# A list scheduler's cost table replaced, and four gate temporaries handed on in a fixed order

## The chip, the core and the metric

The kernel runs on one core of a Trainium2 chip. Five engines with queues of their own work side by side: PE (matrix products, and beside it PEld, the loading of weights), DVE (VectorE), ACT (ScalarE), POOL (GpSimd) and SP, which here issues the transfers. Each engine takes its instructions in the order in which the program lists them, and an instruction that needs another engine's result waits for a semaphore. The metric is the time of one execution on the device, in microseconds, and lower is better. The profile is of one such execution.

## The reference

Inputs are `x` (128 graphs, 128 nodes, 256 features), `adj` (128 x 128 x 128, 0 or 1) and weights. Two layers, each a normalisation and a residual around a graph network. Cut to what matters:

```python
# layer 0: gated graph network, 3 steps
h = relu(layernorm(x)); A = (adj != 0)
for i in range(3):
    m = h @ weight[i]
    aggr = A^T m                          # per graph
    r, z = sigmoid(aggr @ w_ih.T + h @ w_hh.T + biases)   # parts r and z
    n = tanh(i_n + r * h_n)
    h = (1 - z) * n + z * h
x = x + h
# layer 1: one attention layer
h = relu(layernorm(x)); Wh = h @ W; s = Wh.sum(-1)
e = leaky_relu(s[:, :, None] + s[:, None, :], 0.2), -inf where adj == 0
x = x + softmax(e) @ Wh
```

## The kernel before

**Tiling.** Graphs go in 32 groups of four. A group has three state steps (layers 0, 1 and 2 in the code), and then its attention. The features of a group stand as a tile of 128 partitions x 2 x 512 (`hT`), or by rows of nodes (`rows`).

**One state step.** `edge_sums` adds up the neighbours' states: for each half k of the features a batch of 12 small bf16 matmuls (the states are split into three bf16 parts so that nothing is lost) into a PSUM bank of the tag `misc`, and an ACT copy out of it (L626) into `aT`. `node_sums` forms the sums `hs` and `gs` of blocks (on POOL for the state, on DVE for the edges, L666 to L670) that a multiplication scheme with seven products instead of eight needs. `products` then issues these products on PE (L697; in the third step L711, by rows), into the bank pairs X, Y and Q (`x_rz`, `x_n`, `y_rz`, `y_n`, `q_rz`, `q_n`). Y is emptied three times on the way: `put` (L743, L747, L749, ACT) copies it to the temporaries T2 and T3 in SBUF (tags `t2_rz`, `t2_n`, `t3_rz`, `t3_n`), and `add` (L753, DVE) adds Q to them. The gates (`gru`, L799 to L832, or `gru_rows` in the third step, L849 to L893) read X, Y, T2 and T3. In the third step and from the second group on, states are turned between the two layouts by 16-bit halves: an ACT copy into planes (L559), a DMA transpose on SP's queue (L569), an ACT copy back (L563). `parts_of` and `turned_parts` make the bf16 parts on POOL (L580, L583, L600, L605).

**Attention.** `attention` normalises (L503 to L519), forms the scores on DVE (L1022, L1044 to L1050), takes the exponential on ACT (L1055), turns the matrix by DMA (L1164) and multiplies on PE: `weighted` (L652), then the product with the weights (L1088), two graphs to a `misc` bank, which DVE empties as it updates x (L1097). There are two `misc` banks for everything that isn't a product of the state steps.

**What sets the order.** Nothing runs when it is written. Every operation is handed to `Plan.op` with its engine, a cost in ns, what it reads and writes, and a flag `two` if it uses the ports that DVE and POOL share (all of POOL's have it). `Plan.run` then simulates the engines and gives out one order. At each step it takes, for every engine, those operations that could start first, chooses among them the one with the lowest rank (latest start that still meets all due times behind it), and of the engines the one that starts first. The state products (with `due`) are in `bound`: their order is fixed by their due times, and only other PE work is placed between them. `LAG` is the time between the end of an operation and the start of one on another engine that needs it; for transfers it is the flight. `port` is the time from which the shared ports are free. `MARGIN` (7000) makes work that a product needs urgent 7 us early. Between kinds of buffers there is this difference: a "free" buffer goes to whichever operation comes to it first; a "turn" buffer goes from owner to owner in the order of the steps (`waiting`), and the owner's operations get, by the list `after`, a rank that the next owner's first operation sets. The steps of several groups are interleaved: in the middle of the run a round is layer 0 of group g, layer 1 of g-1 and layer 2 of g-2, with the attention of an earlier group beside them.

Of the kernel before, what the change touches and what calls it, by code (L numbers as in the profile page):

```python
# [13 lines left out]
OP = mybir.AluOpType  # L14
# [3 lines left out]
G = 4  # L18
# [23 lines left out]
class Plan:  # L42
# [7 lines left out]
    LAG = {"PE": 250, "ACT": 300, "DVE": 300, "POOL": 300, "SP": 4000}  # L50
# [20 lines left out]
    def op(self, eng, ns, fn, reads=(), writes=(), room=(), due=None, mark=None,  # L71
           turn=None, two=False, lag=None):
# [24 lines left out]
        for b in free:  # L97
# [3 lines left out]
                           two or eng == "POOL", self.LAG[eng] if lag is None else lag])  # L101
# [4 lines left out]
        if turn is not None:  # L106
            self.turns.append((i, turn))

    def run(self):
# [29 lines left out]
        def rank_all():  # L139
            for i in reversed(topo):  # L140
                eng, ns, due = nodes[i][0], nodes[i][1], nodes[i][5]
                gap = 0 if i in bound else MARGIN
                rank[i] = min([due] + [rank[u] - (0 if nodes[u][0] == eng != "SP" else nodes[i][7])
                                       - (gap if u in bound else 0) for u in after[i]]) - ns
# [15 lines left out]
        clock, port = dict.fromkeys(self.LAG, 0.0), 0.0  # L160
# [3 lines left out]
        while len(order) < len(nodes):  # L164
            best = None
            for e, pool in ready.items():
                if not pool:
                    continue
                starts = []
                for i in pool:  # L170
                    if i in bound and i != chain[-1]:
                        continue
                    t = max(clock[e], at[i], port if nodes[i][6] else 0.0)
                    for b in nodes[i][4]:
                        if b.slot is None:
                            t = max(t, min(slots[b.tag]))
                            if b.tag in waiting and waiting[b.tag][-1] is not b:
                                t = float("inf")
                    starts.append((t, i))
                first = min((t for t, _ in starts), default=float("inf"))  # L180
                if first == float("inf"):
                    continue
                i = min((i for t, i in starts if t <= first), key=lambda i: (rank[i], i))
                if best is None or first < best[0]:
                    best = (first, e, i)
            t, e, i = best
# [4 lines left out]
            clock[e] = t + n[1]  # L191
            if n[6]:
                port = clock[e]
            end = max(end, clock[e])
            for b in n[4]:
# [6 lines left out]
                b.done = max(getattr(b, "done", 0.0), clock[e] + n[7])  # L202
                if not b.left:
                    slots[b.tag][b.slot[1]] = b.done
            for u in users[i]:
                missing[u] -= 1
                at[u] = max(at[u], clock[e] + (0 if nodes[u][0] == e != "SP" else n[7]))
                if not missing[u]:
                    ready[nodes[u][0]].append(u)
# [6 lines left out]
def kernel(  # L216
# [54 lines left out]
        "t2_rz": (1, "free", work, [P, 2, H]), "t2_n": (1, "free", work, [P, 2, H]),  # L271
        "t3_rz": (1, "free", work, [P, 2, H]), "t3_n": (1, "free", work, [P, 2, H]),
# [225 lines left out]
    def normed(src, dst, lo=0, hi=G):  # L498
# [3 lines left out]
        for b in range(lo, hi):  # L502
            op("DVE", 415, lambda b=b: nc.vector.bn_stats(ap(st)[:, b, :], ap(src)[:, b, :]),  # L503
               [(src, b, b + 1)], [(st, b, b + 1)])
# [4 lines left out]
        op("DVE", 160 * (hi - lo), aggr, [st], [mv])  # L509

        def rstd():
# [3 lines left out]
        op("DVE", 170, lambda: nc.vector.scalar_tensor_tensor(  # L515
            ap(nm)[:, part], ap(mv)[:, part, 0], -1.0, ap(rs)[:, part], op0=OP.mult, op1=OP.mult),
           [mv, rs], [nm])
        for b in range(lo, hi):
            op("ACT", 520, lambda b=b: nc.scalar.activation(  # L519
# [31 lines left out]
    def turned_halves(src, rows, dst):  # L551
# [5 lines left out]
        for k in range(KD):  # L557
# [5 lines left out]
            op("ACT", 1340, lambda k=k: nc.scalar.copy(  # L563
# [3 lines left out]
    def transpose(pl, plT, k, n):  # L567

        op("SP", 100, lambda: nc.sync.dma_start_transpose(  # L569
            ap(plT)[:, k, 0:n].rearrange("p c (m q) -> p (c m) q", q=P),  # L570
            ap(pl)[:, k, 0:n].rearrange("p c m -> p (c m)")), [(pl, k, k + 1)], [(plT, k, k + 1)],
           lag=4500)

    def parts_of(rows):
# [3 lines left out]
        for n in range(2):  # L578
            part = slice(2 * n, 2 * n + 2)
            op("POOL", 1106, lambda part=part: nc.gpsimd.tensor_tensor(  # L580
                ap(r1)[:, part], ap(rows)[:, part], top(rows)[:, part], OP.subtract),
               [(rows, 2 * n, 2 * n + 2)], [(r1, n, n + 1)])
            op("POOL", 1050, lambda part=part: nc.gpsimd.tensor_tensor(  # L583
# [5 lines left out]
    def turned_parts(hT):  # L589
# [6 lines left out]
        for k in range(KD):  # L596
# [3 lines left out]
            op("POOL", 1150, lambda k=k, r=r: nc.gpsimd.tensor_tensor(  # L600
# [4 lines left out]
            op("POOL", 1150, lambda k=k, r=r: nc.gpsimd.tensor_tensor(  # L605
# [5 lines left out]
    def edge_sums(parts, a, dst):  # L611
# [5 lines left out]
        for k in range(KD):  # L617
# [7 lines left out]
            op("PE", 700, edges, reads(k) + [a], [ps], [dst])  # L625
# [18 lines left out]
    def weighted(m, a, dst, lo, hi, homes):  # L644

        n, cols = hi - lo, slice(lo * N, hi * N)
        for k in range(KD):
# [7 lines left out]
            op("PE", 225 * n, sums, [(m, lo, hi), (a, lo, hi)], [ps], [dst])  # L655
# [60 lines left out]
    def products(layer, hT, hs, aT, gs, rows=False):  # L716
# [23 lines left out]
        def put(t, y, bias=None, mark=None):  # L740
# [9 lines left out]
            op("ACT", 760, halves, [y, W["bias_n"]], [t], mark=mark)  # L750
# [37 lines left out]
    def gru(layer, hT, hs, aT, gs):  # L788
# [7 lines left out]
        for j, n, src in blocks:  # L796
            cr, cz, cn, i = j, KD + j, 2 * KD + j, 2 * j + n
            s_rz, nn = src["rz"], src["n"]
            op("ACT", 511, lambda j=j, n=n, s_rz=s_rz, c=cr: nc.scalar.activation(  # L799
                view(rz, 0)[:, j, n, :], ap(s_rz)[:, 0, :], AF.Tanh, bias=ap(W["bias_s"])[:, c:c + 1],  # L800
                scale=0.5), [s_rz, W["bias_s"]], [(rz, i, i + 1)])
            if src is X:
                op("DVE", 290, lambda j=j, n=n: nc.vector.tensor_scalar(
                    view(rz, 0)[:, j, n, :], view(rz, 0)[:, j, n, :], 1.0, None, op0=OP.add),
                   [], [(rz, i, i + 1)])
                op("DVE", 480, lambda j=j, n=n, nn=nn: nc.vector.scalar_tensor_tensor(
                    view(u)[:, j, n, :], ap(nn)[:, 0, :], ap(W["bias_n"])[:, 0:1], view(rz, 0)[:, j, n, :],
                    op0=OP.add, op1=OP.mult), [nn, (rz, i, i + 1), W["bias_n"]], [(u, i, i + 1)])
            else:
                op("DVE", 480, lambda j=j, n=n, nn=nn: nc.vector.scalar_tensor_tensor(  # L810
# [6 lines left out]
            op("ACT", 500, lambda j=j, n=n, s_rz=s_rz, c=cz: nc.scalar.activation(  # L817
# [18 lines left out]
    def gru_rows(layer, hT, hs, aT, gs, rows, x1):  # L836
# [6 lines left out]
        for j, n, src in blocks:  # L843
            i = 2 * n + j
            outs = slice(j * P, (j + 1) * P)
            for m, bank in enumerate((src["rz"], src["n"])):
                graph, unit_of = 2 * n + m, 2 * i + m
                sbuf = bank.tag[0] == "t"
                op("ACT", 390, lambda outs=outs, graph=graph, bank=bank: nc.scalar.activation(  # L849
# [3 lines left out]
                op("DVE", 290, lambda outs=outs, graph=graph, bank=bank: nc.vector.scalar_tensor_tensor(  # L853
# [4 lines left out]
                op("DVE", 290, lambda outs=outs, graph=graph, bank=bank: nc.vector.scalar_tensor_tensor(  # L858
                    view(u)[:, graph, outs], view(u)[:, graph, outs], 0.5, flat(bank)[:, 3 * P:4 * P],
                    op0=OP.mult, op1=OP.add), [bank], [(u, unit_of, unit_of + 1)], two=sbuf)  # L860
        for n in (1, 0):
# [5 lines left out]
            tanh = [723, lambda cols=cols: nc.scalar.activation(  # L867
# [19 lines left out]
            op("POOL", 1290, lambda cols=cols, part=part: nc.gpsimd.tensor_tensor(  # L887
# [20 lines left out]
    def group(g):  # L908
# [4 lines left out]
        for t, src, kb in ((rows0, x[graphs].rearrange("b n d -> n b d"), 512),  # L913
                           (at, adj[graphs].rearrange("b n m -> n b m"), 256)):
            if g < TIMED:
                load(t, ap, src, kb, lag=4800 if t is at else 3300)
            else:
                op("SP", 100, lambda t=t, src=src: nc.sync.dma_start(ap(t), src), [], [t])
        op("DVE", 420, lambda: nc.vector.tensor_scalar(ap(a), ap(at), 0.0, None,
                                                       op0=OP.not_equal), [at], [a])  # L920
        plan.due = (phase(g, L - 1) + 2) * SLOT
        normed(rows0, rows0)
        for layer in range(L):
# [9 lines left out]
            else:  # L933
# [3 lines left out]
                op("SP", 100, lambda: nc.sync.dma_start(  # L937
                    ap(x1), x[graphs].rearrange("b n d -> n b d")), [], [x1])
            hs, aT, gs = buf("hs"), buf("aT"), buf("gs")
            node_sums(hT, hs, "POOL", 1390, 940)  # L940
            edge_sums(parts, a, aT)
            node_sums(aT, gs, "DVE", 690, 440)
# [12 lines left out]
    def edges_of(g, a):  # L955

        e = buf("e")
        op("DVE", 415, lambda: nc.vector.tensor_scalar(
            ap(e), ap(a), 0.0, -BIG, op0=OP.is_equal, op1=OP.mult), [a], [e])
        return e, (buf("s_all") if g >= NG - ENDING else e)  # L960

    def attention(g, scores, x1, h1, lo, hi):
# [8 lines left out]
        for b in range(lo, hi):  # L971
            hw = buf("hw")
            op("DVE", 520, lambda b=b, hw=hw: nc.vector.scalar_tensor_tensor(
# [65 lines left out]
        if ending:  # L1039
            op("DVE", cost, lambda: nc.vector.tensor_reduce(small(top), sums(), AX.X, OP.max), units, [top])  # L1040
            op("DVE", 260, bound, [s], [top, low])
            op("ACT", 320 * n, leaky, [s] + units, [(e, lo, hi)])
# [17 lines left out]
        op("ACT", (400 if ending else 320) * n, exps, [low],  # L1060
# [39 lines left out]
        op("SP", 100, lambda: nc.sync.dma_start(  # L1100
# [35 lines left out]
    def by_graph(g, lo, hi, exps, e, low, den, rden, rows_w, x1):  # L1136
# [3 lines left out]
        for b in range(lo, hi):  # L1140
            i = b - lo
            op("ACT", 400, lambda b=b: exps(b, b + 1), [low], [(e, b, b + 1), (den, b, b + 1)])
# [12 lines left out]
            op("SP", 100, lambda b=b: nc.sync.dma_start(out[g * G + b], ap(x1)[:, b]), [(x1, b, b + 1)], [])  # L1155
# [4 lines left out]
    def turned_halves_of(halves, src, dst):  # L1160
# [3 lines left out]
        op("SP", 100, lambda: nc.sync.dma_start_transpose(  # L1164
            ap(peT).rearrange("p two g q -> p (two g) q"),
            ap(pe).rearrange("p two g m -> p (two g m)")), [pe], [peT])
        op("ACT", 1340, lambda: nc.scalar.copy(halves_of_blocks(dst), ap(peT)), [peT], [dst])
# [36 lines left out]
```

## Time and profile before

| | us |
|---|---|
| three runs | 2105.02, 2105.40, 2105.88 |
| their median | 2105.40 |
| span of the profiled execution | 2103.8 |
| PE, time in which some matmul is under way | 2084.5 |
| PE, first matmul starts | 1.25 |

The profiled span runs from the first to the last instruction of the program, and what lies around it is part of the time of a run, so the two differ by 1.6 us. A matmul instruction of 128 x 256 in f32 shows a duration of 0.38 us, but one starts every 0.216 us, since they overlap; one of 128 x 384 starts every 0.323 us, a bf16 one of 128 x 128 every 0.056. So a PE that is busy all the time may still not be full, and the starts are what counts. Every f32 product appears as two instructions.

In the middle of the run the pattern repeats with each round of three state steps. The page's busy shares of an engine are over the whole span; for a question about one place, the stretch tables (busy us of each engine between two times) and the chain of waits are of more use. "Waits" give the engine and line that waited, the one waited for, the sum in us, how often, and the longest.

### The profile page before, as it was taken

To read this page: it belongs to the slowest core of one execution; us is meant where nothing else is said; L and a number is where in the kernel's file an instruction comes from. 1 tells how busy PE (TensorE), PEld (TensorE's weight loads), DVE (VectorE), ACT (ScalarE), POOL (GpSimd) and SP (SyncE) were. 2 spreads that over 40 slices of the span, in tenths; PEclk is the share of its full clock that TensorE was granted. 3 is DMA by queue.
4 is the path that set the end of the run, shared out by engine and by line. 5 is a ranking of instruction groups with operands and counts; after the bars stand their busy time and mean duration, and the time that the engine had idled before them with its cause. 6 is when DMAs were issued, how large, how long until landed. Compare 5 with 4: busy or idle time off the path is not lost.

```text
span 2103.8 us, 30718 instructions
## 1 busy us (share of the span) xinstructions
PE 2084.5 (99%) x10624; PEld 1661.6 (79%) x10624; DVE 1714.1 (81%) x3626; ACT 1612.9 (77%) x2977; POOL 923.7 (44%) x881
## 2 busy tenths in 40 slices
PE   8999999999999999999999999999999999999998
PEld 6886887777887778887778877778877788688765
DVE  6767888788888888888888887888878978778788
ACT  5577887877878787877778777778787777677676
POOL 4544554344443435543444543444444454335330
PEclk9999999999999999999999999999999999999999
DMA  4322323322233222323223233222323222312231
GB/s 131 61 51 48 56 54 81 67 54 61 68 73 81 60 58 65 72 70 76 61 56 70 68 73 68 54 61 68 74 61 85 45 62 71 76 41 61 56 71 41
DMA packets 365148, 137.02 MB, mean 65 GB/s; under 512 B 296384, under 2 KB 364736, under 8 KB 364992
## 3 DMA queue, kind: packets, MB, share of 16 engines
q1 hardware_dynamic: 364992, 135.05, 28.8%
q8 instruction: 84, 1.38, 0.3%
q14 instruction: 72, 0.59, 0.1%
HBM read 45.36 MB, written 16.78 MB: 30 GB/s over the span
## 4 chain that ended last, share of the span: by engine, by line
PE 94%; DVE 3%; ACT 1%; DMA 1%; issue 0%; SPq 0%; DVEq 0%; ACTq 0%
PE y_rz L697 15%; PE q_rz L697 10%; PE x_rz L697 10%; PE y_n L697 8%; PE misc L623 6%; PE y_n L711 5%; PE y_rz L711 5%; PE x_n L697 5%; PE q_n L697 5%; PE misc L1088 5%; PE q_rz L711 4%; PE x_n L711 4%; PE x_rz L711 4%; PE q_n L711 4%; PE misc L652 3%; PE misc L452 0%
## 5 line engine op out<-in xcount | busy, mean ns | idle before, releaser
L580 POOL TENSOR_TENSOR r<-rows 128x512 f32<-128x512 f32 x126 | 139.7, 1129 | 295.9 <-ACT rows L563 201.7
L743 ACT COPY t_rz<-y_rz 128x512 f32<-128x512 f32 x192 | 112.5, 586 | 130.4 <-PE y_rz L697 91.8
L666 POOL TENSOR_TENSOR hs<-hT 128x512 f32<-128x512 f32 x96 | 126.6, 1319 | 190.7 <-PE y_n L711 110.9
L753 DVE TENSOR_TENSOR t_rz<-t_rz,q_rz 128x512 f32<-128x512 f32 x192 | 131.5, 685 | 86.5 <-ACT t_rz L743 43.5
L697 PE MATMUL y_rz<-hs,s_hh 128*128 128x256 f32 x768 | 197.4, 379 | 0.6 <-ACT t_rz L743 0.5
L697 PE MATMUL y_rz<-gs,s_x 128*128 128x256 f32 x768 | 197.1, 379 | 0.0
L670 POOL TENSOR_TENSOR hs<-hT,hs 128x256 f32<-128x256 f32 x96 | 77.5, 807 | 209.6 <-PE q_n L711 169.2
L697 PEld LDWEIGHTS y_rz<-gs,s_x 128*128 128x128 f32 x768 | 145.9, 190 | 19.8
L605 POOL TENSOR_TENSOR pl<-d,pl 128x512 bf16<-128x512 f32 x64 | 76.1, 1193 | 191.9 <-ACT pl L603 191.7
L697 PEld LDWEIGHTS y_rz<-hs,s_hh 128*128 128x128 f32 x768 | 143.5, 190 | 20.0 <-ACT t_rz L743 1.4
L583 POOL TENSOR_TENSOR p<-r 128x512 bf16<-128x512 f32 x126 | 156.7, 1262 | 0.0
L753 DVE TENSOR_TENSOR t_n<-t_n,q_n 128x512 f32<-128x512 f32 x192 | 131.2, 683 | 30.4 <-PE q_n L711 13.0
L666 DVE TENSOR_TENSOR gs<-aT 128x512 f32<-128x512 f32 x96 | 87.8, 914 | 54.3 <-ACT aT L626 53.7
L697 PE MATMUL x_rz<-aT,s_x 128*128 128x256 f32 x512 | 131.4, 379 | 0.0
L697 PE MATMUL x_rz<-hT,s_hh 128*128 128x256 f32 x512 | 131.4, 379 | 0.0
L600 POOL TENSOR_TENSOR d<-hT,pl 128x512 f32<-128x512 f32 x64 | 82.6, 1293 | 97.2 <-ACT pl L598 91.5
L626 ACT COPY aT<-misc 128x512 f32<-128x512 f32 x190 | 110.4, 586 | 17.7 <-PE misc L623 13.0
L1088 PE MATMUL misc<-w,uT 128*128 128x256 f32 x480 | 115.1, 383 | 3.1 <-DVE x L1097 2.3
L697 PE MATMUL y_n<-hs,s_hh 128*128 128x256 f32 x384 | 114.3, 379 | 0.0
L697 PE MATMUL y_n<-gs,s_x 128*128 128x256 f32 x384 | 114.2, 379 | 0.0
L697 PEld LDWEIGHTS x_rz<-hT,s_hh 128*128 128x128 f32 x512 | 97.2, 190 | 19.3
L887 POOL TENSOR_TENSOR x<-x,u 128x512 f32<-128x512 f32 x60 | 79.4, 1342 | 69.8 <-DMA x<-in_x_dram 42.1
(286 smaller groups left out, 6324.4 us busy)
## 6 DMA issues: line engine op xcount, KB each, us to landing
rows<-in_x_dram SPq DMA_DIRECT2D x32, 512.0 KB, 4.2
x<-in_x_dram SPq DMA_DIRECT2D x32, 512.0 KB, 3.9
out_dram<-x SPq DMA_DIRECT2D x31, 512.0 KB, 2.9
at<-in_adj_dram SPq DMA_DIRECT2D x32, 256.0 KB, 2.8
plT<-pl SPq DMA_TRANSPOSE x186, 3.3
peT<-pe SPq DMA_TRANSPOSE x60, 3.1
e<-in_L_gnn_weight_dram SPq DMA_DIRECT2D x3, 256.0 KB, 3.1
rz<-in_L_gnn_w_ih_dram SPq DMA_DIRECT2D x2, 384.0 KB, 4.3
```

The lines of the kernel that those rows point to most:

```text
L580: op("POOL", 1106, lambda part=part: nc.gpsimd.tensor_tensor(ap(r1)[:, part], ap(rows)[:, part], top(rows)[:, part], OP.subtract), [(rows, ...
L583: op("POOL", 1050, lambda part=part: nc.gpsimd.tensor_tensor(ap(p3)[:, part], ap(r1)[:, part], top(r1)[:, part], OP.subtract), [(r1, n, n ...
L600: op("POOL", 1150, lambda k=k, r=r: nc.gpsimd.tensor_tensor(ap(r), ap(hT)[:, k], part(pl, k, 0), OP.subtract), [(hT, 2 * k, 2 * k + 2), (p ...
L623: nc.tensor.matmul(flat(ps)[:, b * N:(b + 1) * N], part(i, b, k), ap(a)[:, b, :], start=(i == 0), stop=(i == 2))
L626: op("ACT", 590, lambda k=k, ps=ps: nc.scalar.copy(ap(dst)[:, k, :], flat(ps)), [ps], [(dst, 2 * k, 2 * k + 2)])
L666: op(eng, cost, lambda: sub(ap(w)[:, 0:2, :], blocks()[:, 1::2, :], blocks()[:, 0:2, :], OP.subtract), [t], [(w, 0, 2)], two=True)
L697: nc.tensor.matmul(ap(bank)[:, half, :], ap(w)[:, i - 1, gate, :], source(i, t, sums), start=(first and c == 0 and m == 0), stop=False, sk ...
L711: op("PE", 645, lambda c=c, w=w, t=t, sums=sums: nc.tensor.matmul(flat(bank)[:, c * P:(c + 3) * P], source(i, t, sums)[:, m * N:(m + 1) * ...
L743: op("ACT", 590, lambda: nc.scalar.copy(ap(t), ap(y)), [y], [t], mark=mark)
L753: op("DVE", 690, lambda: nc.vector.tensor_tensor(ap(t), ap(t), ap(q), OP.add), [q], [t])
L887: op("POOL", 1290, lambda cols=cols, part=part: nc.gpsimd.tensor_tensor(part(x1), part(x1), ap(u)[:, cols], OP.add), [(u, 2 * lo, 2 * hi)] ...
L1088: nc.tensor.matmul(ap(ps)[:, b, :], ap(uT)[:, k, (m + b) * N:(m + b + 1) * N], ap(w1)[:, k, :], start=(k == 0), stop=(k == KD - 1))
```

## The change

The edit replaces the numbers with which the planner thinks, changes its rules in four places, and turns the four temporaries from "free" to "turn". The arithmetic and the set of instructions stay; what can differ is their order and in which of two equal buffers something stands.

1. Lags: `LAG` of an operation becomes what passes before its result is there (PE 163, SP 3600, 0 for the others), and `SIGNAL` adds the time that the waiting engine takes to see it. New `Plan.wait(i, u)` joins them; only between two PE operations is it zero, so operations of one engine that depend on each other have a gap too.
2. `OVER`: an engine is free for its next operation before the one under way is done (ACT 103 ns, DVE 84, POOL 42).
3. `thin` and `FLIP`: a PE operation that isn't thin starts 56 ns later behind one that is. The bf16 batches of `edge_sums` are thin.
4. `HANDOFF`: the shared ports are free 120 ns before an operation on them is done; and among engines that could start at the same time, the one whose operation asked first gets the turn.
5. Costs of single operations, and more DVE operations marked as users of the ports (`two`): L515, L803, L919 and L958.
6. Transfers: a transpose costs SP 1283 with a flight of 2200 (before 100 and 4500), other transfers 480 (before 100); the few timed loads at the start keep theirs.

```diff
-    LAG = {"PE": 250, "ACT": 300, "DVE": 300, "POOL": 300, "SP": 4000}
+    LAG = {"PE": 163, "ACT": 0, "DVE": 0, "POOL": 0, "SP": 3600}
+    OVER = {"PE": 0, "ACT": 103, "DVE": 84, "POOL": 42, "SP": 0}
+    FLIP, HANDOFF = 56, 120
+    SIGNAL = {"PE": 53, "ACT": 36, "DVE": 36, "POOL": 78, "SP": 28}
...
+    def wait(self, i, u):
+
+        a, b = self.nodes[i], self.nodes[u][0]
+        return 0 if a[0] == b == "PE" else a[7] + self.SIGNAL[b]
...
-                rank[i] = min([due] + [rank[u] - (0 if nodes[u][0] == eng != "SP" else nodes[i][7])
+                rank[i] = min([due] + [rank[u] - self.wait(i, u)
                                        - (gap if u in bound else 0) for u in after[i]]) - ns
...
-                    t = max(clock[e], at[i], port if nodes[i][6] else 0.0)
+                    t = max(clock[e] + (self.FLIP if thin and e == "PE" and not nodes[i][8] else 0), at[i])
...
-                    starts.append((t, i))
-                first = min((t for t, _ in starts), default=float("inf"))
+                    starts.append((max(t, port) if nodes[i][6] else t, t, i))
+                first = min((t for t, _, _ in starts), default=float("inf"))
...
-                i = min((i for t, i in starts if t <= first), key=lambda i: (rank[i], i))
-                if best is None or first < best[0]:
-                    best = (first, e, i)
-            t, e, i = best
+                asked, i = min(((r, i) for t, r, i in starts if t <= first), key=lambda x: (rank[x[1]], x[1]))
+                if best is None or (first, asked) < best[:2]:
+                    best = (first, asked, e, i)
+            t, _, e, i = best
...
-            clock[e] = t + n[1]
+            done = t + n[1]
+            clock[e] = done - self.OVER[e]
             if n[6]:
-                port = clock[e]
-            end = max(end, clock[e])
+                port = done - self.HANDOFF
+            if e == "PE":
+                thin = n[8]
+            end = max(end, done)
...
-                b.done = max(getattr(b, "done", 0.0), clock[e] + n[7])
+                b.done = max(getattr(b, "done", 0.0), done + n[7] + 36)
...
-                at[u] = max(at[u], clock[e] + (0 if nodes[u][0] == e != "SP" else n[7]))
+                at[u] = max(at[u], done + self.wait(i, u))
...
-        "t2_rz": (1, "free", work, [P, 2, H]), "t2_n": (1, "free", work, [P, 2, H]),
-        "t3_rz": (1, "free", work, [P, 2, H]), "t3_n": (1, "free", work, [P, 2, H]),
+        "t2_rz": (1, "turn", work, [P, 2, H]), "t2_n": (1, "turn", work, [P, 2, H]),
+        "t3_rz": (1, "turn", work, [P, 2, H]), "t3_n": (1, "turn", work, [P, 2, H]),
...
-        op("SP", 100, lambda: nc.sync.dma_start_transpose(
+        op("SP", 1283, lambda: nc.sync.dma_start_transpose(
...
-           lag=4500)
+           lag=2200)
...
-            op("PE", 700, edges, reads(k) + [a], [ps], [dst])
+            op("PE", 671, edges, reads(k) + [a], [ps], [dst], thin=True)
...
-                op("DVE", 480, lambda j=j, n=n, nn=nn: nc.vector.scalar_tensor_tensor(
+                op("DVE", 422, lambda j=j, n=n, nn=nn: nc.vector.scalar_tensor_tensor(
```

The other costs, line by line (before, after; `n` is the number of graphs): L503 415, 412; L508 160n, 85+65n; L515 170, 155; L519 520, 592; L563 and L1167 1340, 1347; L580 1106, 1042; L583 1050, 1042; L600 and L605 1150, 1158; L652 225n, 223n; L747 with L749 760, 728; L799 511, 496; L803 290, 278; L806 480, 485; L817 500, 495; L849 390, 403; L853 and L858 290, 286; tanh in `gru_rows` (L867) 723, 630; L887 1290, 1273; `node_sums` on POOL 1390 and 940, then 1272 and 730, its halves on DVE 440, 426; L958 415, 420; L973 520, 432; L1031 320n, 100+285n; L1055 320n (400n in the last two groups), 100+290n (100+390n); the exponential of the last group, by graph, 400, 480; L918, L937, L1100 and L1155 100, 480.

## The prediction

> **What bounds the kernel now.** I read the page first (busy shares, then the slices), then stretches of 64 us, then the waits of PE, and last the chain of waits in the one stretch that stood out.
>
> The busy shares of the page:
>
> ```profile
> PE 2084.5 (99%) x10624; PEld 1661.6 (79%) x10624; DVE 1714.1 (81%) x3626; ACT 1612.9 (77%) x2977; POOL 923.7 (44%) x881
> ```
>
> The stretches (length, then busy time of PE, PEld, DVE, ACT, POOL, clock, DMA share, GB/s):
>
> ```profile
> 0.00:64.00 64.00, 58.38 (x303) 46.51 (x304) 45.09 (x98) 38.84 (x80) 36.38 (x42) 1.00 0.40 113
> ...
> 615.72:679.58 63.86, 63.86 (x330) 51.23 (x329) 51.18 (x116) 51.05 (x95) 26.46 (x27) 1.00 0.33 71
> 679.58:743.44 63.86, 63.86 (x330) 51.23 (x329) 54.38 (x112) 49.65 (x91) 30.31 (x29) 1.00 0.29 66
> ...
> 1796.00:1815.00 19.00, 14.63 (x41) 8.91 (x40) 15.79 (x31) 9.39 (x19) 5.54 (x4) 0.82 0.33 97
> ...
> 2048.00:2104.00 56.00, 48.27 (x218) 32.63 (x216) 45.78 (x140) 35.08 (x86) 6.48 (x8) 0.98 0.17 48
> ```
>
> The reader is to see two things. A round of three state steps takes 63.86 us, and PE is busy in all of them: in the middle of the run there is no hole to close, and the change takes no matmul away. And holes are in few places: 5.6 us in the first 64, 7.7 in the last 56, 4.4 in the 19 us from 1796, where the clock is also below full. The longest waits of PE say the same:
>
> ```profile
> PE misc L1088 <- DVE x L1097: 2.3, 1, 2.3
> PE y_n L711 <- ACT t_n L743: 2.0, 1, 2.0
> PE misc L533 <- DVE h L360: 1.3, 1, 1.3
> PE misc L441 <- DMA e<-in_L_gnn_weight_dram: 1.3, 1, 1.3
> ```
>
> The first two belong to the stretch at 1796; its chain of waits (start us, us, what) shows why:
>
> ```profile
> 1793.78 1.15 DVE gs L670
> 1794.92 1.18 DVE u L810
> 1796.10 0.61 DVE e L1022
> 1796.71 0.02 issue
> 1796.74 1.54 DVE e L1044
> ...
> 1798.30 1.54 DVE e L1046
> ...
> 1801.59 3.66 PE misc L1088 x8
> ```
>
> VectorE works through the attention scores in order, and the update of x (L1097) that frees the misc bank for PE stands behind them. L810 takes 0.42 us elsewhere in this stretch and L1044 0.76 on the mean of 30; here they take twice that or more, beside GpSimd's L580, L583 and L600.
>
> **What the Trainium skill says.** "SBUF — State Buffer", section "Who interferes with whom": a VectorE instruction with two SBUF inputs and a GpSimd instruction that reads SBUF share ports, and the later one blocks wholly. The 1.54 us above agrees, and so does L1048, a reduction with one input, at 0.69 us beside them. "TensorE: Matmul & The Clock Gate", section "What's actually happening": the clock falls to half after an idle window of about 3.4 us and comes back after a busy one. Here two stretches of 3.3 us (from 1801.8 and 1808.7) show 0.50, after waits of only 2.35 and 2.03 us, so a shorter wait is enough. No page bears on an f32 matmul behind a bf16 one; the trace gives that below.
>
> **The change part by part.**
>
> *Matmul flips (thin, FLIP).* In the PE timeline the first f32 matmul behind a bf16 batch is 53 to 56 ns longer (median 55); there are 148 such places, 8.2 us in all. An edge sum is two batches of 12, k=0 and k=1, and often a product stands between them. The planner now charges 56 ns to whatever follows a thin batch unless it is thin too, so a ready thin batch goes first whatever its rank. Following the planner's dependencies through the trace, at 50 of the 148 places the next thin batch already had its inputs and its bank. 50 x 56 ns = 2.8 us less, on PE itself, so nothing hides it. Bounds: 0, if banks are held longer in the new order, and 148 x 56 = 8.3. I take 2.8. The product that steps back does so by 0.67 us (12 x 56 ns), beside full work on PE.
>
> *The jam at 1796.* It costs 2.35 + 2.03 us of waiting; the eight L1088 take 3.65 us and not 1.89 (1.76 more), the x and n products after it 1.48, 1.48 and 1.17 and not 0.81 each (1.70 more). Sum 7.8 us. The new planner knows VectorE's and GpSimd's durations better (L810 from 480 to 422, L1044 as before, L580 from 1106 to 1042), gives the port up 120 ns before an operation ends, gives it to the one that asked first, and marks L515, L803, L919 and L958 as users of it. It also lets a VectorE instruction start 84 ns before the one ahead is done and an ACT one 103, so that side work is planned earlier (in the VectorE timeline L810 does start at 1789.68, 80 ns before L832, begun at 1789.07 and 0.69 long, ends). A jam that needs four port collisions in a row is an accident of one order; in a re-made order I expect it gone more often than not. Bounds: 7.8 gained, or none; I take 7.8. If it goes, what is late next is the q_rz product at 2033 (0.7 us), which I leave.
>
> *Lags.* ACT and DVE results were planned 300 ns late, now 36 or, to PE, 53. The trace supports this: where PE waited, it started 52 to 55 ns after the releaser ended. No instruction is added, and a cover of 0.25 us that the order had for free goes. In the round from 615.72, the closest release is that of y_rz at 642.13: its bank was emptied by an ACT copy that ended at 641.69, so 0.44 us early; the next ones are 0.9 and 1.1. I cost this at nothing, covered by those margins; without them, see the slower rival.
>
> *DMA.* A transpose was planned as 100 + 4500 ns, now 1283 + 2200 and 36 for the signal, 3.52 us. The trace has 3.0, 3.3 and 5.1 us (least, median, most) for the 186 of plT. All are on SP's queue, which also carries the rows, adjacency and output transfers; each SP step now holds its queue 480 or 1283 ns in the plan, as it does on the chip (a transpose's issue takes 1.27). The reading copies (L563, L1167) stand in ACT's queue; one that is early blocks the bank-emptying copies behind it, by up to 5.1 - 3.5 = 1.6 us. Nothing for the median, and for the slow tenth (over 4.0 us) 0.5 us, about the smallest margin. I take 0, with 0 to 10 us (0.45 in each of 23 rounds) as bounds.
>
> *Set order for t2/t3.* Each of the four is one buffer and in use by one step at a time; steps are already made in the order of their phases, so the hand-over sequence is the same. New is that VectorE's and ACT's work that frees a buffer takes its urgency from the next step that writes it. No instruction, no wait on PE that is not there now: 0, with 1 us either way as bounds, about one more or one fewer of the waits of 0.7 to 1.3 us that PE has now.
>
> *The two ends.* The first 64 us wait for weights and first rows, the last 56 for the last group's softmax. Both are chains of data; I take 0, with 2 us either way for each.
>
> Sum: 2103.8 - 2.8 - 7.8 = 2093.2 us span. The three runs of before have a median of 2105.4, 1.6 above the profiled span, so **2094.8**.
>
> **Rivals.**
>
> A, the forecast (0.52): flips and jam go. 2089 to 2099, from the ends' 2 us each and two new waits of about 2.
>
> B, the jam stays or another of its size takes its place (0.22): 2105.4 - 2.8 = 2102.6. For it: DVE has 81% and the last groups run in another order of phases, where ports collide most; nothing in the change moves the attention chain off VectorE. Against it: one case in the trace.
>
> C, slower (0.20): the evictions become late in every round. Place: ACT's copies of the y banks (L743) behind a transpose copy that waits, and PE's y products behind them. The smallest margin is 0.44 us; a copy later by 1.4 leaves PE waiting 0.95 in each of the 23 like rounds between 300 and 1760 us: 21.9 us. With A's 10.6 gained: 2105.4 + 11.3 = 2116.7. It cancels the gain from 0.46 us a round (10.6 / 23), and is slower by more than can be mistaken from 0.64. For it: landings up to 5.1 us and the planned 300 ns gone. Against: ACT is busy 51 of 63.86 us, and 90% of the landings come within 4.0.
>
> D, it does not do what it says (0.06): the fixed order of products carries the rest, the batches stay apart, the jam stays: 2105.4.
>
> **How the numbers follow.** The smallest difference that a measurement of this kernel can tell from none is 0.2%, 4.2 us: faster is below 2101.2, slower above 2109.6. Faster: 0.50 of A and 0.07 of B (another small stall gone beside the flips), 0.57. Same: 0.02 of A, 0.13 of B, D, and 0.01 of C, 0.22. Slower: 0.02 of B and 0.19 of C, 0.21. The range is 2088 to 2110: it takes in A, B and D with their unknown costs, and leaves out most of C (0.17) and 0.03 below. Likeliest alone: 2089 to 2099.
>
> **What would show it.** Flips: 95 to 100 places where f32 follows bf16, with the k=0 and k=1 batches as one group of 24 in the timeline, and rounds of about 63.75 us. Jam: PE busy throughout 1780 to 1830, clock 1.00. C: PE's waits show L743 ahead of y products 20 times or more, and PE in a middle round below 63.8 busy us. I am wrong if PE's holes move to the middle of the run, or if a wait of over 2 us and a half clock stand anywhere between 64 and 2040.

## The result and the profile after

The changed kernel takes 2112.7 us (median of five runs, 2111.3 to 2113.3), the kernel before 2105.0 beside it: a ratio of 1.0038, interval 1.0026 to 1.0050. It is slower, where 2094.8 was forecast. Its profiled span is 2110.9 us, 7.0 longer than before.

The busy shares of its page, then the stretch tables (from and to, length, busy time of PE, PEld, DVE, ACT, POOL, clock, DMA share, GB/s):

```profile
PE 2084.3 (99%) x10624; PEld 1658.4 (79%) x10624; DVE 1680.2 (80%) x3626; ACT 1594.6 (76%) x2977; POOL 921.5 (44%) x881
```

```profile
0.00:64.00 64.00, 59.02 (x304) 47.34 (x305) 44.43 (x97) 37.86 (x80) 38.82 (x45) 1.00 0.38 108
647.06:711.83 64.77, 64.09 (x329) 51.14 (x328) 53.01 (x112) 49.86 (x93) 28.36 (x27) 1.00 0.28 65
711.83:776.61 64.78, 64.07 (x329) 51.13 (x328) 53.03 (x112) 49.85 (x93) 28.37 (x27) 1.00 0.29 66
1780.00:1830.00 50.00, 50.00 (x266) 39.21 (x265) 39.56 (x82) 43.47 (x80) 27.77 (x25) 1.00 0.23 45
2048.00:2110.00 62.00, 56.42 (x250) 38.51 (x248) 48.26 (x157) 38.17 (x93) 4.66 (x8) 1.00 0.18 53
```

The page's shares look like those of before, and would hide the change. The stretches don't: the jam near 1800 us is gone, with PE busy throughout and the clock at 1.00, but a round in the middle takes 64.78 us instead of 63.86, with a hole of 0.7. The waits of PE name it:

```profile
PE y_rz L722 <- ACT t_rz L754: 14.1, 19, 1.3
PE q_n L1160 <- DVE eT L1158: 1.4, 1, 1.4
```

(Lines have moved by 7 to 11: L722 is L711 of before, the product of the third step by rows; L754 is L743, the copy that empties a Y bank.) It comes in 19 of the 20 rounds between 300 and 1600 us.

A full account comes from the starts of PE's matmuls: the distance from each start to the next, less that of an unhindered one of its shape (0.216 us for 128 x 256, 0.323 for 128 x 384, 0.056 for bf16, 0.112 and 0.429 for the f32 ones of 128 and 512 columns). What is left over, in us, with the flips apart:

| | before | after | e1_swap | e5_split | e10_split553 |
|---|---|---|---|---|---|
| flips (f32 behind bf16) | 8.1 | 5.5 | 5.5 | 5.5 | 5.4 |
| 0 to 64 us | 8.6 | 9.3 | 10.4 | 10.6 | 8.2 |
| 64 to 300 | 1.1 | 1.2 | 2.0 | 0.9 | 0.3 |
| 300 to 1600 | -1.5 | 20.2 | 1.9 | 0.9 | -1.5 |
| 1600 to 2000 | 9.3 | 0.3 | 0.5 | 0.3 | -0.4 |
| 2000 to the last matmul | 8.2 | 4.6 | 4.5 | 5.1 | 3.8 |
| ahead of the first and behind the last | 5.6 | 5.3 | 5.3 | 6.1 | 5.3 |
| span | 2103.8 | 2110.9 | 2094.5 | 2093.8 | 2085.6 |

(A little below zero is in the shapes' medians. The three columns on the right are experiments.) So the change gained 2.6 us of flips, 9.0 between 1600 and 2000, and 3.9 at the end, and lost 21.7 in the rounds and 0.8 before them: 7.0 in sum.

Why the copy is late is read from one round. ACT's timeline before the wait at 648.22 us (start, length, instruction; the bracket is idle time of the engine and who ended it):

```profile
643.51 0.72 ACT L834 ACTIVATE u<-u,bias_i 128x512 f32<-128x512 f32 x1 [1.40 <-DVE u L825]
644.14 0.57 ACT L668 COPY uT<-misc 128x512 f32<-128x512 f32 x1
644.61 2.08 ACT L530 ACTIVATE h<-x,nm,rs 128x256 f32<-128x256 f32 x4
646.64 1.04 ACT L570 COPY pl<-hT 128x1024 uint16<-128x1024 uint16 x1
647.59 0.58 ACT L754 COPY t_rz<-y_rz 128x512 f32<-128x512 f32 x1
```

VectorE's and then GpSimd's timeline in the same round, and PE's:

```profile
641.87 1.28 DVE L679 TENSOR_TENSOR gs<-gs,aT 128x256 f32<-128x256 f32 x1
643.07 0.41 DVE L825 SCALAR_TENSOR_TENSOR u<-u,t_n 128x256 f32<-128x256 f32 x1
643.40 0.41 DVE L681 TENSOR_TENSOR gs<-aT,gs 128x256 f32<-128x256 f32 x1
```

```profile
641.71 1.16 POOL L616 TENSOR_TENSOR pl<-d,pl 128x512 bf16<-128x512 f32 x1 [2.40 <-ACT pl L614]
```

```profile
648.22 0.91 PE L722 MATMUL y_rz<-s_hh,hs 128*128 128x384 f32 x2 [0.68 <-ACT t_rz L754]
```

GpSimd's L616 began 0.16 us ahead of VectorE's L679, which takes 1.28 us here, while L681, of the same shape, takes 0.41 shortly after. Behind it comes L825, ACT's tanh (L834) waits for that, and behind the tanh stand 3.7 us of work (L668, four L530, L570) that PE's next product doesn't need; only then comes the copy that it waits for. Every link of this is an engine's own order.

But this meeting was in the plan. `Plan.run` gives each operation a start (`t` in its code), and these starts can be set beside the trace, operation by operation. Just ahead of the wait PE runs 11.04 us behind its planned times; "on PE's count" below is a planned time plus that. The plan has L679 wait behind L616 and end at 642.26 on PE's count. It ended at 643.15, so VectorE was 0.9 us late, but it had been so before: the tanh of 635.97 is 0.92 late. What the plan did not have lies ahead of that tanh, on GpSimd and VectorE:

```profile
633.15 1.45 POOL L677 TENSOR_TENSOR hs<-hT 128x512 f32<-128x512 f32 x1
634.68 1.06 POOL L679 TENSOR_TENSOR hs<-hs,hT 128x256 f32<-128x256 f32 x1
```

```profile
633.40 1.75 DVE L840 SCALAR_TENSOR_TENSOR d<-rz,d 128x512 f32<-128x512 f32 x1
635.52 0.42 DVE L825 SCALAR_TENSOR_TENSOR u<-u,y_n 128x256 f32<-128x256 f32 x1
635.86 1.23 DVE L843 SCALAR_TENSOR_TENSOR hT<-d,u 128x512 f32<-128x512 f32 x1
```

```profile
635.97 0.72 ACT L834 ACTIVATE u<-u,bias_i 128x512 f32<-128x512 f32 x1 [1.60 <-DVE u L825]
```

GpSimd's first node sum of the state (L677) was planned behind VectorE's L840, at 634.10 on PE's count; it began 0.95 us sooner, ahead of L840. L840 and L843, planned at 0.69 us each, took 1.75 and 1.23 beside the sums. From there on VectorE and ACT stay about 0.9 us late. And the plan has only 0.15 us between the end of the copy (L754) and the start of the product (L722), 0.05 of it for the signal.

### The profile page after: what moved, and what is told of

Its sections match the earlier page's. It is cut to its first block, busy times and chain, and to the rows that moved or that the text cites. A ratio compares the mean times of both kernels' runs of the same rounds, so it can differ in the third digit from the quotient of the medians.

```text
span 2110.9 us, 30632 instructions
## 1 busy us (share of the span) xinstructions
PE 2084.3 (99%) x10624; PEld 1658.4 (79%) x10624; DVE 1680.2 (80%) x3626; ACT 1594.6 (76%) x2977; POOL 921.5 (44%) x881
## 4 chain that ended last, share of the span: by engine, by line
PE 79%; ACT 10%; DVE 7%; issue 2%; DMA 0%; POOL 0%; SPq 0%; DVEq 0%; ACTq 0%; POOLq 0%
PE y_rz L708 14%; PE x_rz L708 10%; PE q_rz L708 8%; PE y_n L708 7%; PE y_rz L722 5%; PE misc L1099 5%; PE y_n L722 5%; PE misc L634 5%; PE x_n L708 4%; PE q_n L708 4%; PE q_rz L722 3%; PE x_n L722 3%; PE x_rz L722 3%; PE q_n L722 3%; ACT h L530 2%
## 5 line engine op out<-in xcount | busy, mean ns | idle before, releaser
L677 POOL TENSOR_TENSOR hs<-hT 128x512 f32<-128x512 f32 x96 | 129.5, 1350 | 304.5 <-PE y_n L722 238.9
L754 ACT COPY t_rz<-y_rz 128x512 f32<-128x512 f32 x192 | 112.2, 584 | 146.4 <-PE y_rz L708 136.1
L708 PE MATMUL y_rz<-hs,s_hh 128*128 128x256 f32 x768 | 200.0, 383 | 1.0 <-ACT t_rz L754 0.9
L708 PE MATMUL y_rz<-gs,s_x 128*128 128x256 f32 x768 | 197.1, 379 | 0.0
L708 PEld LDWEIGHTS y_rz<-hs,s_hh 128*128 128x128 f32 x768 | 142.8, 190 | 27.1 <-ACT t_rz L754 9.2
L708 PEld LDWEIGHTS y_rz<-gs,s_x 128*128 128x128 f32 x768 | 145.9, 190 | 19.8
L681 POOL TENSOR_TENSOR hs<-hT,hs 128x256 f32<-128x256 f32 x96 | 75.3, 785 | 177.1 <-PE q_n L722 160.7
L834 ACT ACTIVATE u<-u,bias_i 128x512 f32<-128x512 f32 x128 | 92.8, 725 | 74.0 <-DVE u L825 73.8
L708 PE MATMUL x_rz<-hT,s_hh 128*128 128x256 f32 x512 | 131.4, 379 | 0.0
L708 PE MATMUL x_rz<-aT,s_x 128*128 128x256 f32 x512 | 131.4, 379 | 0.0
L840 DVE SCALAR_TENSOR_TENSOR d<-rz,d 128x512 f32<-128x512 f32 x128 | 117.6, 920 | 0.9
L637 ACT COPY aT<-misc 128x512 f32<-128x512 f32 x190 | 102.8, 581 | 18.1 <-PE misc L634 17.9
L616 POOL TENSOR_TENSOR pl<-d,pl 128x512 bf16<-128x512 f32 x64 | 75.7, 1183 | 89.9 <-ACT pl L614 89.8
L708 PE MATMUL y_n<-gs,s_x 128*128 128x256 f32 x384 | 114.3, 379 | 0.0
L708 PE MATMUL y_n<-hs,s_hh 128*128 128x256 f32 x384 | 114.3, 379 | 0.0
L837 DVE TENSOR_TENSOR d<-hT,u 128x512 f32<-128x512 f32 x128 | 107.3, 839 | 8.5 <-ACT u L834 6.3
```

Source lines behind the costliest of these rows:

```text
L637: op("ACT", 590, lambda k=k, ps=ps: nc.scalar.copy(ap(dst)[:, k, :], flat(ps)), [ps], [(dst, 2 * k, 2 * k + 2)])
L677: op(eng, cost, lambda: sub(ap(w)[:, 0:2, :], blocks()[:, 1::2, :], blocks()[:, 0:2, :], OP.subtract), [t], [(w, 0, 2)], two=True)
L708: nc.tensor.matmul(ap(bank)[:, half, :], ap(w)[:, i - 1, gate, :], source(i, t, sums), start=(first and c == 0 and m == 0), stop=False, sk ...
L754: op("ACT", 590, lambda: nc.scalar.copy(ap(t), ap(y)), [y], [t], mark=mark)
L837: op("DVE", 690, lambda j=j, d=d, cols=cols: nc.vector.tensor_tensor(ap(d), ap(hT)[:, j, :], ap(u)[:, cols], OP.subtract), [(hT, lo, hi), ...
L840: op("DVE", 690, lambda d=d, cols=cols: nc.vector.scalar_tensor_tensor(ap(d), ap(rz)[:, 1, cols], 1.0, ap(d), op0=OP.add, op1=OP.mult), [( ...
```

## The experiments

All ran beside the kernel before, whose median in the three sets was 2102.7, 2104.5 and 2103.0 us. Edits are to the changed kernel unless said otherwise. Theory S: the copies are planned without room, so any lateness of VectorE reaches PE. Its rivals: D, transposes that land late (rival C of the prediction); T, the set order of the temporaries; and P, which says where VectorE's lateness is from.

**The suspected order alone (e1_swap).** At the end of `run`:

```diff
+        for q, p in zip(acts, acts[1:]):
+            if nodes[q][1] == 1045 and nodes[p][1] == 590 and any(b.tag == "t2_rz" for b in nodes[p][4]) \
+                    and all(order_at[u] > order_at[p] for u in users[q]):
+                order.remove(q)
+                order.insert(order.index(p) + 1, q)
```

> The changed kernel with one edit of its order: where ACT's copy into the planes (1045 ns, of the turned halves) stands just ahead of the copy that empties y_rz into t2_rz, it goes behind it. Theory S (the T2 copy is planned just in time behind other ACT work, and VectorE's lateness passes through it to PE): the waits of PE's y_rz product on that copy (0.7 us and a slow restart, 18 times) go, rounds fall from 64.8 to 63.7-63.9 us, the time to about 2095 (2093 to 2099). If the copy is late for its own input (PE's earlier y product, or a DMA ahead of it), the swap changes nothing: 2112.

Measured: 2095.5 us, ratio 0.9963 (0.9948 to 0.9978). A round, and ACT's timeline at the place:

```profile
644.70:708.50 63.80, 63.80 (x329) 51.17 (x329) 51.95 (x113) 49.69 (x93) 28.56 (x27) 1.00 0.30 66
```

```profile
641.96 0.72 ACT L841 ACTIVATE u<-u,bias_i 128x512 f32<-128x512 f32 x1 [1.40 <-DVE u L832]
...
645.03 0.57 ACT L761 COPY t_rz<-y_rz 128x512 f32<-128x512 f32 x1
645.50 1.05 ACT L577 COPY pl<-hT 128x1024 uint16<-128x1024 uint16 x1
```

The tanh still waits 1.40 us for VectorE; only the copy stands one place earlier, and the waits are gone. The edit makes this exchange 24 times, about once in a round. One instruction of ACT, 1.05 us long and ahead of the copy, cost 16.4 us of the span over the run (2110.9 to 2094.5). That the copy stood behind it without room is the shown cause of the loss; why VectorE was late is the next question.

**The set order undone (e2_free).** The four tags "free" again.

> The changed kernel with the four temporaries as before (free instead of in turn), the new numbers kept. Theory T (the set order gives VectorE's and ACT's work a new urgency, and that put other work ahead of the copy): the wait at the y_rz product goes, about 2095. Theory S: the numbers cause it, and just-in-time copies appear with either kind of buffer, at the same place or another: 2105 to 2120, with waits of 0.3 to 1.5 us in each round.

Measured: 2124.3 us, ratio 1.0102 (1.0087 to 1.0117). The waits move to the Y products of the first two steps (L708):

```profile
PE y_rz L708 <- ACT t_rz L754: 17.8, 22, 3.4
```

Theory T falls: without the set order it is the same kind of wait at another place, and the time is longer, by 11.6 us between the medians (which are of different sets) and by 14.4 between the profiled spans.

**More room for PE (e3_signal1053).** `SIGNAL = {"PE": 1053, ...}`.

> The changed kernel with SIGNAL to PE 1053 instead of 53: everything PE needs is planned to be there 1 us earlier. Theory S: VectorE runs 0.9 to 1.2 us later than planned, so 1 us of planned slack takes up nearly all of it: PE's waits in the rounds shrink to under 0.2 us, time 2094 to 2099. Theory D (late transposes): landings up to 1.6 us over plan; waits shrink but some of 0.5 us stay, 2098 to 2105. Theory T: no change, 2110 to 2114.

Measured: 2099.6 us, ratio 0.9984 (0.9977 to 0.9992), just outside S's 2094 to 2099. In the rounds no wait is left (the account has -1.3 us from 300 to 1600). Theory S holds there; the total is dulled by a wait of 5.0 us for VectorE's gs sums near 2030 us, with a stretch at half clock behind it (the pair after the wait takes 1.65 us instead of 0.81), which the new order brought.

**Transposes as before (e4_transposes).** 100 with a flight of 4500 instead of 1283 and 2200.

> The changed kernel with the transposes' cost and flight as before (100 + 4500 ns instead of 1283 + 2200). Theory D (rival C as the prediction put it: ACT's reading copies wait for transposes that land later than planned): the wait at the y_rz product goes, 2094 to 2099. Theory S: ACT doesn't wait for transposes there; the order is another one, but PE's waits in the rounds stay of the same kind, 2105 to 2120.

Measured: 2118.6 us, ratio 1.0070 (1.0053 to 1.0089). PE's waits:

```profile
PE y_rz L722 <- ACT t_rz L754: 10.7, 22, 0.8
PE y_rz L708 <- ACT t_rz L754: 3.8, 10, 0.5
```

The wait stays at the same product. D's expectation fails: transposes planned as late as before don't take the wait away.

**GpSimd's starts known to the planner (e5_split).** In this kernel `hs` is one tile of four blocks. The planner holds a buffer until its last reader is done, and the last reader is the last product of a step; but the first node sum writes two blocks alone, whose readers are done several products earlier, and on the chip it starts then. (In the changed kernel the sum of 608.94 us began 0.12 us after the last reader of its two blocks had ended, and 5.1 us ahead of the end of the tile's last reader.) With three tiles of the same bytes the planner sees what the chip does:

```diff
-        "hs": (2, "turn", work, [P, 4, H]), ...
-        "gs": (2, "turn", work, [P, 4, H]),
+        "hs": (2, "turn", work, [P, 2, H]), "hs2": (2, "turn", work, [P, 1, H]),
+        "hs3": (2, "turn", work, [P, 1, H]), ...        # and gs, gs2, gs3 alike
-        op(eng, cost, lambda: sub(ap(w)[:, 0:2, :], ... [t], [(w, 0, 2)], two=True)
+        op(eng, cost, lambda: sub(ap(w[0])[:, 0:2, :], ... [t], [w[0]], two=True)
```

> The changed kernel with each of hs and gs in three tiles (two, one and one of its four blocks) instead of one, the same bytes and the same operations. The planner keeps a buffer taken until its last reader is done, while on the chip GpSimd may write the first two blocks as soon as their own readers are; with three tiles it plans with that. Theory P (GpSimd starts its sums earlier than planned, meets VectorE at the shared ports at times nobody planned, and that makes VectorE late): VectorE's late steps in the round get fewer, and the wait at the y products falls from 0.87 us with its restart to under 0.3, time 2094 to 2101. If the lateness has another source, waits of 0.5 to 1.3 us a round stay somewhere: 2105 to 2120.

Measured: 2094.6 us, ratio 0.9949 (0.9932 to 0.9965). The page, and ACT at the same place of the round:

```profile
PE 2078.7 (99%) x10624; PEld 1663.6 (79%) x10624; DVE 1615.4 (77%) x3626; ACT 1594.7 (76%) x2977; POOL 916.8 (44%) x881
```

```profile
639.26 0.58 ACT L670 COPY uT<-misc 128x512 f32<-128x512 f32 x1 [1.28 <-PE misc L665]
639.75 2.08 ACT L532 ACTIVATE h<-x,nm,rs 128x256 f32<-128x256 f32 x4
641.73 1.04 ACT L572 COPY pl<-hT 128x1024 uint16<-128x1024 uint16 x1
642.80 0.58 ACT L756 COPY t_rz<-y_rz 128x512 f32<-128x512 f32 x1
```

The four instructions stand in the same order as in the changed kernel, and yet PE doesn't wait. It is another order all the same: the tanh (L836, at 636.76) now stands well ahead of them, and nothing near them waits for VectorE. Meetings at the ports are not gone either: VectorE's first gs sum of this round (636.91) takes 1.27 us, but the plan has it wait there. The same 3626 VectorE instructions are busy 64.8 us less (1680.2 to 1615.4). Reductions with one input keep their length (L1074 of the changed kernel 684 ns, L1076 here 685), while one with two inputs from SBUF falls from 920 ns (L840) to 719 (L842), so this is less time spent waiting at the ports.

Plan and trace side by side, from 300 to 1600 us and for operations of a single instruction, show what the split did (times in us, on PE's count; "tight" are the copies of Y to T2 that the plan lets end less than 0.2 ahead of a y_rz product of the third step):

| | changed kernel | e1_swap | e5_split |
|---|---|---|---|
| tight copies in the plan, and the median distance to the product | 20, 0.15 | 20, 0.15 | 19, 0.18 |
| their end against the plan, median | 0.96 late | 0.07 early | 0.27 early |
| GpSimd's first sum of the state ahead of its plan, median | 5.1 | 4.9 | 0.0 |
| VectorE operations ended over 0.5 late | 797 of 2002 | 1050 of 2027 | 84 of 2028 |

(The plan of e1_swap is the one ahead of its exchange.) The plan is as tight in all three. In e1_swap VectorE is as late as ever, and the copy in time because it was moved; in e5_split GpSimd starts as planned, and VectorE and the copy are in time. So theory P holds for the changed kernel: node sums that GpSimd began ahead of the plan made VectorE late. Two things had to come together, a plan without room and a start that the plan had wrong.

**Room for ACT's results alone (e6_act1000).** `wait` gets 1000 ns more from ACT to PE.

> The changed kernel with 1000 ns more between ACT's results and PE alone (53 stays from VectorE and GpSimd). Theory S: the y copies are what is planned too tightly, so the rounds are free of waits as with 1053 for all, and the 5 us wait for VectorE's gs sums near the end of that run needn't be there: 2091 to 2097. If VectorE's results are too tight for PE as well, waits for DVE show up in the rounds: 2098 to 2110.

Measured: 2102.5 us, ratio 0.9991 (0.9985 to 0.9998). The rounds are as free of waits as in e3 (-1.3 us from 300 to 1600), but 7.3 us are lost from 64 to 300 and 11.2 at the end. The part on the rounds holds, the time (2091 to 2097) doesn't.

**The flips alone (e7_thin_only).** The kernel before with `thin` and `FLIP`.

> The kernel before with thin and FLIP alone. Flips fall from 148 to about 100, 2.7 us less on PE. Theory S: with the old lags of 250 to 300 ns the rounds have no wait, 63.7 us each; the jam near 1800 us may stay or go: 2102 with it, 2094 without. If pairing the edge batches itself makes the y copies late, rounds are 64 us or more: over 2107.

Measured: 2100.7 us, ratio 0.9983 (0.9975 to 0.9990). Flips cost 6.3 us instead of 8.1, less of a gain than in the full change; the rounds are clean (-1.2), and the jam is gone (1.7 from 1600 to 2000). In its place a product waits 2.5 us for ACT near 2053. The time is still not the 2094 expected without the jam: 4.0 us are lost from 64 to 300 us (1.1 before) and 9.4 at the end (8.2 before). So pairing the batches did no harm in the rounds, and a small edit to the planner was enough for an order without the jam.

**The old lags (e8_lag_old).** `LAG` of before, `OVER`, `HANDOFF` and `SIGNAL` zero, the rest of the change kept.

> The changed kernel with LAG as before (250, 300, 4000), OVER, HANDOFF and SIGNAL at zero, the new costs, thin, the marks of port users and the set order kept. Theory S: 300 ns of planned lag on ACT's and VectorE's results, and the operations planned without overlap, leave room again; waits in the rounds under 0.3 us, 2094 to 2103. If the new costs or marks made the order tight, waits at the y products stay: 2106 to 2120.

Measured: 2121.0 us, ratio 1.0077 (1.0062 to 1.0092). This was a miss. The Y copies no longer stand first, but 18.9 us are lost from 300 to 1600 at the misc banks, to ACT's copies (L637) and VectorE's updates (L1108). The old lags with the new costs and marks make another order, worse in another way; which of them does it isn't shown. S's expectation failed here, and since the waits are mostly at other places, the run tells little on the copies.

**The split without the change (e9_before_split).** The kernel before, with the tiles of e5.

> The kernel before with hs and gs in three tiles each, as in the run e5_split, and nothing else. If the jam near 1800 us came from GpSimd's unplanned starts, it goes: 2096 to 2098 (7.8 less, flips stay at 148). If it is an accident of the order whatever the planner knows of GpSimd, the order changes and the time lies anywhere from 2096 to 2110. VectorE's busy time against before: theory P expects it lower (under 1690 us).

Measured: 2107.8 us, ratio 1.0026 (1.0016 to 1.0036). VectorE is busy 1716.4 us, not less than before (1714.1), and the stretch from 1600 to 2000 loses 9.1 us as it did, in another wait: 5.9 us of a y_rz product for its copy, at 1777. P's expectation for VectorE missed here. With the old numbers the split doesn't make the plan right: GpSimd's first sum of the state still begins over 0.5 us ahead of it in 44 of 61 cases between 300 and 1600 us. And something else than the jam's wait can cost the same at that place.

**Both remedies (e10_split553).** e5 with `SIGNAL` to PE 553.

> e5_split with SIGNAL to PE 553 instead of 53. Theory S and P together: with GpSimd planned well, VectorE is at most 0.1 us later than planned at the y copies, so half a microsecond of room is enough and takes away the one wait of 0.7 left at 325 us: 2092 to 2095. If the room costs more at the end of the run than it saves in the rounds (as the 5 us wait with 1053 did): 2095 to 2100.

Measured: 2087.0 us, ratio 0.9923 (0.9907 to 0.9940), faster than expected and the fastest of all. Page and one round:

```profile
PE 2074.6 (99%) x10624; PEld 1662.1 (80%) x10624; DVE 1592.3 (76%) x3626; ACT 1594.7 (76%) x2977; POOL 924.1 (44%) x881
```

```profile
640.00:703.70 63.70, 63.70 (x330) 51.25 (x329) 48.29 (x112) 49.91 (x93) 28.98 (x27) 1.00 0.29 67
```

How much room the copies have is seen from the other side, ACT's waits for the third step's Y product (sum, times): where ACT waits for PE, the copy is in time. Before, after, and in this run:

```profile
ACT t_rz L743 <- PE y_rz L711: 37.8, 42, 4.5
```

```profile
ACT t_rz L754 <- PE y_rz L722: 9.9, 12, 2.1
```

```profile
ACT t_rz L756 <- PE y_rz L724: 52.9, 44, 3.4
```

The change took this from 42 times to 12, half a microsecond of planned room with the split gave 44. In this plan no copy of Y to T2 or T3 is tight in the third step any more: the least distance there is 1.77 us between 300 and 1600.

**The split without the set order (e11_split_free).**

> e5_split with the four temporaries free as before. If the set order is worth nothing of its own once GpSimd is planned well: 2093 to 2097. If it is what keeps the y copies in time (with one tile hs it was 2124 without it): waits at y_rz in the rounds, 2105 to 2125.

Measured: 2100.6 us, ratio 0.9987 (0.9980 to 0.9994), between the two expectations: 6.0 us over e5 between the medians of two sets, 4.4 between the profiled spans, 8 if each is set against the kernel before that ran beside it. With the split, too, the kernel with the set order is the faster one, by less than without it (11.6 and 14.4, e2 against the changed kernel). How much of this is the set order and how much the accident of a new order isn't shown.

## Why the prediction was wrong

*Flips: right.* 2.8 us forecast, 2.6 measured, at 100 places left of 149.

*The jam: right in size, thin in reason.* 7.8 us forecast, 9.0 gained from 1600 to 2000. That it is an accident of one order is borne out: of the twelve orders run (e1_swap left out), four others (e2, e4, e8, e9) lose 4 to 12 us in the same stretch, and seven lose 3 or less. That it went is thus partly luck. One reading of the lines was wrong: L1048 was named as a one-input reduction that keeps its 0.69 us beside GpSimd's work, but it began at 1799.86, when GpSimd's L600 had ended (1796.01 and 3.27 us) and L605 not yet begun (1804.04), so it shows nothing on the ports.

*Lags: the step that failed.* "I cost this at nothing, covered by those margins". The margins of 0.44, 0.9 and 1.1 us were read off the order of before and treated as if they stayed while the lags shrank. They don't belong to the kernel but to the order. The smallest was for the most part the lag itself: the plan of before has 0.38 us between that copy and its product, of which 0.30 is the old `LAG` of ACT. Without that lag nothing keeps 0.30 us free, and the changed plan, with 53 ns for the signal, leaves 0.15 at such places. What stood there instead was a wait of 0.68 us that made nearly every round about 1.0 us longer; 21.7 us were lost from 300 to 1600 us, where nothing was forecast. A hint was in the change itself: fewer nanoseconds in a lag are less room, and the trace of before showed VectorE late by up to 0.85 us at ports (the 1.54 us of L1044), twice the smallest margin.

*DMA: nothing against it.* 0 forecast; e4 doesn't remove the wait. No run isolates its worth.

*Set order: wrong in size, without harm.* 0 and 1 us either way forecast; with it the changed kernel is faster by 12 to 14 us, and with the split by 4 to 8. That it gives urgency to what frees a buffer was said, and its worth left out.

*The ends: one within the bounds, one outside.* 2 us either way; 0.7 lost in the first 64 us, 3.9 gained at the end.

*Rival C was the one that came,* at its place (the Y products of the third step, in nearly every round) with its sign (19 such waits there and two in the earlier steps, where 20 or more were named) and near its price (21.9 us forecast, 21.7 measured), but behind another instruction: not a transpose's reading copy, but four normalisations and the copy into planes, after a wait for VectorE. That the price agrees is luck: C had a copy 1.4 us late against a margin of 0.44, in 23 rounds, and it was 0.96 late against 0.10 to spare, in 19. With A's gains nearer 15 than 10.6 it came to 2112.7, not 2116.7. Forecast A is what the changed kernel gives with one ACT instruction moved in each round: 2095.5 for 2094.8.

What stays open: why just this order came out, that is, which of the new costs put the other work ahead of the copy. No run isolates one. That VectorE's lateness is from GpSimd's early starts rests on the plan beside the trace and on e5, which also makes a new order; no run holds GpSimd back in an order that is otherwise kept.

## What to carry to other kernels

Margins read from a trace belong to the order in that trace, and may be no more than the planner's own lag: when lags are cut, ask what the planner will put into the room, and look at the engine that empties the accumulators first. Set the planner's times beside the trace before you name a culprit; a long instruction can be planned, and a start that is too early can do the harm. Measured durations make a plan tight, and a plan with 0.1 us to spare paid here for an event that it didn't know; give a small planned room (0.5 us here) to what the bound engine waits for, and find what the plan has wrong, here a buffer that is really freed in parts. In a kernel bound by one engine at 99%, look for a wait that repeats in each round; 0.7 us there outweighs a jam of 8.

## What the runs showed that was not expected

A wait costs more than the profile's figure for it: the 0.68 us are 1.0 of the round (64.78 against 63.80). Unhindered, a pair of these matmuls starts 0.65 us after the one before, although that shows a length of 0.81; the wait is counted from the end, so the start comes 0.84 late. And the first pair after the wait took 0.91 us instead of 0.81.

Planned room is not free of side effects, and not in proportion: 1000 ns for ACT alone came to 2102.5, 1000 for all to 2099.6, 500 for all with the split to 2087.0. Each makes another order at the start and the end of the run too.
